# Layer 0 of a four-layer convolution network: an earlier sampling chain, a later copy of the second sum's rows, one more VectorE eviction

## The chip, the cores and the metric

The kernel runs on one core of a Trainium2 chip. The metric is the device time in microseconds (us) of one execution of the whole program, four layers in one launch; the change touches layer 0 alone. Engines are named TensorE (PE, with its weight loads PEld), VectorE (DVE), ScalarE (ACT), GpSimd (POOL) and SyncE (SP, which issues DMAs here).

## The reference

Layer 0 is an attention over sampled keys with a learned position bias, on `x` of shape (2, 512, 32, 32), 8 heads of 64 channels, one group a head:

```python
q = _gconv1x1(xn, qw)
off = tanh(einsum(gelu(depthwise_conv(q) + b), off_pw_w)) * 4.0     # 64 offsets a head
vgrid = grid + off                                                  # where to sample
kv = _grid_sample(xn, vgrid)                                        # bilinear, 64 keys a head
k, v = _gconv1x1(kv, kw), _gconv1x1(kv, vw)
pos = grid_q[:, :, None, :] - grid_kv[:, None, :, :]                # 1024 queries x 64 keys x 2
bias = sign(pos) * log1p(abs(pos))
bias = relu(bias @ cpb_w1 + cpb_b1)                                 # 2 -> 128
bias = relu(bias @ cpb_w2 + cpb_b2)                                 # 128 -> 128
bias = bias @ cpb_w3 + cpb_b3                                       # 128 -> 1
attn = softmax(q^T k * 64**-0.5 + bias)
x = x + out_w @ (attn v);  x = x + mlp(bn2(x))
```

For each of the 16 heads of the two batches, 1024 x 64 positions go through the 128 x 128 layer `cpb_w2`. That is nearly all of layer 0's work. Layers 1 to 3 are other attentions and are the same in both kernels.

## The kernel before

**Units and blocks.** The loop of layer 0 goes over 16 *units* u (a batch and a head), in each over 8 steps o, in each over two halves: 256 *blocks*, written (o,half) below. Two units share one of 8 *pairs* (128 channels); an odd unit is the second of its pair. In a block `first_hidden` (L746) makes four tiles h1 of 128 x 1024 for the **next** block on VectorE (L760), from a buffer that holds two blocks' worth. `second_hidden` (L771) multiplies them by `cpb_w2` on TensorE (L787) into four PSUM tiles of 128 x 1024, called q0 to q3 here. The PSUM pool `ps` has three such tiles, so each one needs the third before it evicted; the transposes of a pair (`tr`, L674) and the attention's output (`o`) take tiles of the same pool.

**Evictions.** ScalarE evicts q0 to q3 with a relu (L801) and scales q0 (L806, with a bias L804). GpSimd then adds the four up: an accumulating DMA y1 += y0 (L811), y3 += y2 (L815), y3 += y1 (L818, one block later, `join`). In some blocks VectorE evicts one tile with the addition in it: q3 in *late* blocks (L796), q2 in *early* ones (L799); in an early block L811 and ScalarE's eviction of q2 fall away, and L806 becomes L804.

**Folds and gathers.** The sum of a step is folded by accumulating DMAs on GpSimd's queue (L821, L843, L846) and *gathered* by two DMAs on SP (`sum<-h`, L853) into `sum0` (even o) or `sum1` (odd o). A unit later these sums are scaled (L222), folded (`keys_rows`, L858 and L861) and copied to the tile `rows` by two DMAs on SP each (`rows<-sum`, L865). `self.refolds` lists all these steps with the block in which each is due, and `refold_more` (L827) takes what is due; its last call in a block (`gather=True`) issues the SP DMAs. The gather of step o is due in block 2o + 5 of the unit, counted from 0, the rows of the first sum in block 6 and those of the second in block 8. In each engine's queue instructions run in the order in which they are issued. On SP the order comes from priorities; a DMA issued inside `self.behind(self.gathered)` stands behind the last gather.

**The attention of the unit before** (`attend`, L905, v = u - 1) starts at block (5,0): VectorE adds `rows` to the scores (L910), transposes, takes maxima, subtracts (L925); ScalarE takes the exponential at the end of block (6,0) (L927); VectorE sums, divides and transposes back (the *division*, L934 and L936) at the end of (7,0); TensorE multiplies by v (L947) at the end of (7,1).

**The next pair's chain** (`offsets`, L401, then `sampled`, L592) makes offsets, reads the sampling spots back from DRAM (`at<-spots`, L495), turns `xT` (L674 and its copy L604), takes distances (L611 on VectorE, L618 and L619 on ScalarE), relus (L623, L624), their product (L626), the sampling matmuls (L633) and keys and values (L647 to L655). It advances by one step, up to its next `yield`, at the end of a block: `self.step(after)` first advances the attention; only where that yields nothing true does `self.step(front)` advance the pair's chain:

```python
                    self.refold_more(i, True)
                    if not self.step(after):
                        self.step(front)
```

So a `yield True` in the attention keeps the pair's chain out of that block. The queues of TensorE, ScalarE, VectorE and GpSimd follow this order exactly.

Of the kernel before, what the change touches and what calls it, by code (L numbers as in the profile page):

```python
# [57 lines left out]
class Net:  # L58
# [40 lines left out]
    def layer0(self):  # L99
# [3 lines left out]
        with ExitStack() as ctx:  # L103
# [45 lines left out]
            with self.tc.manual_schedule(engines=engines):  # L149
# [40 lines left out]
                for i, (u, o, half) in enumerate(quads):  # L190
                    self.half = half
                    if o == 2 and half == 1 and u % 2 == 0 and u // 2 + 1 < BP:
                        nxt = pairs[u // 2 + 1]
                        front += [self.offsets(nxt, u // 2 + 1, ps), self.sampled(nxt, u // 2 + 1, ps)]
                    h1 = ready
                    if i + 1 < len(quads):
                        if quads[i + 1][1:] == (7, 0) and u + 1 < 2 * BP:
                            self.advance(front, lambda: "logs" in pairs[(u + 1) // 2])
                        ready = self.first_hidden(*quads[i + 1], pairs, tables)
                    last_set = u == last and o >= 4  # L200
                    if half == 0:
                        if o == 0:
                            before, sums = sums, []
                        if o % 4 == 0:
                            group = []
                        if i + 2 < len(quads):
                            both = self.two_tiles(f"h2_{u}_{o}3")
                            group.append([both[:, 0, :], both[:, 1, :], both])
                        else:
                            group.append([self.four_rows(f"h2_{u}_{o}{n}3") for n in range(2)])  # L210
                        if o < 2:
                            sums.append(self.four_rows(f"sum{u}_{o}"))
                    self.second_hidden(i, u, o, half, h1, group[-1], i + 1 == len(quads), last_set)
                    if half == 1 and not last_set:
                        end = i + (3 if u == last else 4)
                        self.refolds.append((i + 2, end, end, self.refold(group[-1][2], sums[o % 2], o // 2, u == last)))
                    v = u - 1
                    if half == 0 and o in (1, 2) and 0 <= v < last - 1:
                        z = before[o - 1]
                        if o == 1:  # L220
                            rows = self.soft.tile([P, HF], F32, tag="pt", name=f"rows{v}")
                        nc.scalar.activation(z, z, AF.Copy, scale=self.last_sign)  # L222
                        self.refolds.append((i + 1, i + 4, i + 4, self.keys_rows(z, rows, o - 1)))
                    if half == 1 and o == 2 and v >= 0:
                        sims[v] = ps_s.tile([P, HF], F32, tag="sim", name=f"sim{v}")
                        if v == last - 1:
                            self.sum_product(sims[v], self.thrice, True, before)
                        self.advance(front, lambda: "v" in pairs[v // 2])
                        self.keys_queries(v, pairs[v // 2], sims[v], v < last - 1)
                    if v >= 0 and (o, half) == ((5, 0) if v < last - 1 else (2, 1)):  # L230
                        if v == 8:
                            self.advance(after, lambda: False)
                            att = [apool.tile([P, N], F32, tag=f"att{t}", name=f"att{v}_{t}") for t in range(CT)]
                        after.append(self.attend(v, pairs[v // 2], sims[v], att, ps, rows if v < last - 1 else None))
                        if v % 8 == 7:
                            after.append(self.projection(ps, att, ow, v // 8))
                    elif half == 1 and u == last and o == 5:
                        sims[u] = ps_s.tile([P, HF], F32, tag="sim", name=f"sim{u}")
                        self.sum_product(sims[u], self.twice[:, 16:48], True, sums)
                    elif half == 1 and u == last and o == 7:  # L240
                        self.sum_product(sims[u], self.folded[:, 8:40], False, [one[0] for one in group[:2]])
# [3 lines that stand above are left out]
# [347 lines left out]
    def sampled(self, m, bt, ps):  # L592

        nc = self.nc
        b, t = divmod(bt, CT)
        spots = self.fone.tile([P, 2 * NJ, 2], F32, tag="spots", name=f"at{b}{t}")
        if bt > 0:
            yield  # L600
        self.send(bt == 0, spots, m["spots"].rearrange("k d -> (k d)").partition_broadcast(P))
        if "xT" not in m:
            self.sampling(m, bt)
            nc.scalar.copy(m["xT"], self.turn(m, bt, ps))  # L604
        elif "w" not in m:
            self.sampling(m, bt)
        xnT = m["xT"]
        yield
        wx = self.fone.tile([P, 2 * NJ], F32, tag="wx", name=f"wx{b}{t}")
        w = m["w"]  # L610
        nc.vector.tensor_tensor(  # L611
            w,
            spots[:, :, 1].unsqueeze(1).to_broadcast([P, NB, 2 * NJ]),
            self.ys.unsqueeze(2).to_broadcast([P, NB, 2 * NJ]),
            ALU.subtract,
        )
        yield
        nc.scalar.activation(wx, spots[:, :, 0], AF.Abs, bias=self.grid[:, G_X : G_X + 1])  # L618
        nc.scalar.activation(w, w, AF.Abs)  # L619
        yield  # L620
        yield from self.odd()
        wp = self.bank[:, 384:512]
        nc.scalar.activation(wp, wx, AF.Relu, scale=-1.0, bias=1.0)  # L623
        nc.scalar.activation(w, w, AF.Relu, scale=-1.0, bias=1.0)  # L624
        yield
        nc.vector.tensor_tensor(w, w, wp.unsqueeze(1).to_broadcast([P, NB, 2 * NJ]), ALU.mult)  # L626
        yield
        yield from self.odd()
        kv_ps = self.bank[:, 384:448]
        for n in range(NB):  # L630
            for par in range(2):
                rows = slice(par * DH, (par + 1) * DH)
                nc.tensor.matmul(  # L633
                    kv_ps[rows, :],
                    lhsT=xnT[:, n, rows],
                    rhs=w[:, n, rows],
                    start=(n == 0),
                    stop=(n == NB - 1),
                )
        kv = self.fone.tile([P, NJ], F32, tag="kv", name=f"kv{b}{t}")  # L640
        nc.vector.tensor_copy(kv, kv_ps)
        keys = self.fpool.tile([P, 2, NJ], F32, tag="k", name=f"k{b}{t}")
        nc.gpsimd.memset(keys, 0.0)
        yield
        yield from self.odd()
        k_ps = self.bank[:, 256:320]
        nc.tensor.matmul(k_ps, lhsT=self.l0qkv[:, 1, t, :], rhs=kv, start=True, stop=True)  # L647
        v_ps = self.bank[0:NJ, 384:512]
        nc.tensor.matmul(v_ps, lhsT=kv, rhs=self.l0qkv[:, 2, t, :], start=True, stop=True)
        for par in range(2):  # L650
            rows = slice(par * DH, (par + 1) * DH)
            nc.vector.tensor_scalar(keys[rows, par, :], k_ps[rows, :], DH**-0.5, None, ALU.mult)
        vals = self.fpool.tile([P, P], F32, tag="v", name=f"v{b}{t}")
        nc.vector.tensor_copy(vals[0:NJ, :], v_ps)
        nc.scalar.copy(vals[NJ:P, :], v_ps)  # L655
        m["k"], m["v"] = keys, vals
        yield
# [113 lines left out]
    def second_hidden(self, i, u, o, half, h1, one, final, last_set):  # L771
# [4 lines left out]
        nc = self.nc  # L776
        vec, pool = nc.vector, nc.gpsimd
        late = half == 1 and u > 0 and o in ((1, 2), (1, 2, 3, 4))[u % 2]
        early = half == 1 and 0 < u < 2 * BP - 1 and o in (0, 7)
        ys = []  # L780
        for q in range(4):
            hp = self.ps_h.tile([P, N], F32, tag="ps", name=f"hp_{u}_{o}{half}{q}")
# [43 lines left out]

    def refold_more(self, i, gather=False):  # L827

        going = []
        for at, last, when, fold in self.refolds:  # L830
            if at < last and at <= i and not gather or at == last and when <= i and gather:
                for _ in fold:
                    going.append((at + 1, last, when, fold))
                    break
            else:
                going.append((at, last, when, fold))
        self.refolds = going

    def refold(self, both, to, c, once):

# [14 lines left out]
    def keys_rows(self, z, to, jj):  # L855
# [6 lines left out]
        yield  # L862
        for h in range(2):
            at = h * NJ + jj * 32
            nc.sync.dma_start(to[at : at + 32, :], z[0::4, h * HF : (h + 1) * HF])  # L865

    def sum_product(self, sim, lhsT, start, zs):

# [36 lines left out]
    def attend(self, u, m, sim, att, ps, bias=None):  # L905
# [28 lines left out]
        nc.vector.tensor_tensor(t, t, joint.unsqueeze(2).to_broadcast([P, 2 * NB, W]), ALU.mult)  # L934
        pt = self.soft.tile([P, HF], F32, tag="pt", name=f"pt{u}")
        self.weights_turned = nc.vector.transpose(pt, t.rearrange("p a k -> p (a k)"))  # L936
        yield

        if ps:
            o = ps.tile([P, 2, HF], F32, tag="ps", name=f"o{u}")  # L940
# [1276 lines left out]
```

## Time and profile before

| what | value |
|---|---|
| median of 3 runs | 3203.44 us (3201.72 to 3206.21) |
| the profiled execution | 3206.31 us, its span 3204.6 us |
| loop of layer 0, first to last matmul of L787 | 23.1 to 1883.4 us |
| busy, of the span | PE 99%, DVE 77%, ACT 59%, POOL 74% |
| ScalarE evictions L801 | 950, 1109 ns each |
| VectorE h1 L760 | 1028, 1210 ns each |
| accumulating DMAs L811 | 227, 512 KB each |
| mean granted TensorE clock | 1.000 |

A group's row names line, engine and operation, the tiles out<-in and their shape, the count, then busy time and mean ns, then the idle time of the engine just before and what ended it. A timeline row has start and duration in us, engine, line, operation, tiles and count, and in brackets the idle time before the row and its releaser; `SPq` and `ACTq` are DMAs issued by those engines' queues. TensorE is pipelined: rows give its starts as recorded and its ends as modelled, so a stop is read from the distance of starts.

### The profile page before, as it was taken

How to read it: one execution, taken by the hardware profiler on the slowest of the kernel's cores; microseconds unless marked ns; L12 is line 12 of the kernel's file. 1: busy time of each engine (PE TensorE's matmuls, PEld its weight loads, DVE VectorE, ACT ScalarE, POOL GpSimd, SP SyncE). 2: the span in 40 equal slices, each digit the busy share in tenths (PEclk: the TensorE clock that was granted, in tenths of full speed). 3: DMA queues.
4: the chain of work that ended last, by engine and by line, in shares of the span. 5: the costliest groups of instructions: out<-in, count | busy, mean ns of one | idle time of the engine just before them, and what ended most of it. 6: DMA issues, size and time to landing. Idle time of an engine off the chain costs nothing.

```text
span 3204.6 us, 58752 instructions
## 1 busy us (share of the span) xinstructions
PE 3179.3 (99%) x23956; PEld 1201.3 (37%) x23956; DVE 2471.8 (77%) x2834; ACT 1904.5 (59%) x1985; POOL 2363.7 (74%) x1664
## 2 busy tenths in 40 slices
PE   9999999999999999999999999999999999999999
PEld 4333333233233333233333234444556433455333
DVE  7888988888888688888888766475475689755897
ACT  7887877877787587877777641111221566113662
POOL 7999999999999699999999854342353458534575
PEclk9999999999999999999999999999999999999999
DMA  6797797888878588788878751110000000000001
GB/s 168 162 189 161 156 180 165 162 174 167 164 162 178 101 173 164 162 166 175 165 161 171 163 167 61 40 53 27 1 1 27 14 1 1 15 0 14 1 1 54
DMA packets 96591, 341.92 MB, mean 107 GB/s; under 512 B 19888, under 2 KB 22064, under 8 KB 79216
## 3 DMA queue, kind: packets, MB, share of 16 engines
q0 software_dynamic: 56224, 244.88, 40.1%
q1 hardware_dynamic: 23264, 65.20, 6.1%
q10 hardware_dynamic: 16816, 27.90, 3.2%
q8 instruction: 193, 3.16, 0.4%
q14 instruction: 94, 0.77, 0.1%
HBM read 67.37 MB, written 4.46 MB: 22 GB/s over the span
## 4 chain that ended last, share of the span: by engine, by line
PE 71%; POOL 13%; DVE 9%; DMA 3%; issue 3%; ACT 1%; DVEq 0%; POOLq 0%; ACTq 0%; SPq 0%
PE hp L787 33%; POOL h L818 5%; PE s L1750 5%; PE o L1779 5%; POOL h L815 3%; DVE h L760 3%; DMA h<-h 2%; POOL h L811 2%; PE qk30P L1525 2%; PE qk20P L1525 2%; PE m_0P L1034 1%; PE m_6P L1034 1%; PE m_5P L1034 1%; PE m_3P L1034 1%; PE qk31P L1525 1%
## 5 line engine op out<-in xcount | busy, mean ns | idle before, releaser
L787 PE MATMUL hp<-h,w2s 128*32 128x512 f32 x16384 | 1777.5, 593 | 9.9 <-ACT h L801 5.3
L760 DVE CUSTOM_DVE_ANT_1 h<-tx,bank 128x1024 f32<-128x1024 f32 (+1 forms) x1028 | 1180.6, 1210 | 119.0 <-PE hp L787 80.5
L801 ACT ACTIVATE h<-hp,magb 128x1024 f32<-128x1024 f32 x950 | 1044.9, 1109 | 370.5 <-PE hp L787 314.7
L787 PEld LDWEIGHTS hp<-h,w2s 128*32 128x32 f32 x16384 | 550.2, 110 | 1204.3 <-issue 1100.9
L818 POOL TENSOR_TENSOR h<-h,h 128x1024 f32<-128x1024 f32 x254 | 753.4, 2966 | 35.6 <-DMA h<-h 30.4
L815 POOL TENSOR_TENSOR h<-h,h 128x1024 f32<-128x1024 f32 x209 | 653.7, 3128 | 6.7 <-DVE h L799 5.2
L811 POOL DMA_DIRECT2D h<-h x227 | 316.5, 1394 | 81.4 <-ACT h L801 80.9
L1754 ACT ACTIVATE e<-s 128x1024 f32<-128x1024 f32 x256 | 262.0, 1025 | 181.1 <-PE s L1750 174.2
L1779 PE MATMUL o<-e,v 64*64 64x512 f32 x2048 | 265.2, 589 | 2.2 <-DVE q L1818 2.2
L1750 PE MATMUL s<-q,k 64*64 64x512 f32 x2048 | 265.9, 591 | 0.0
L806 ACT ACTIVATE h<-h,flip 128x1024 f32<-128x1024 f32 x182 | 209.6, 1152 | 6.0
L843 POOL DMA_DIRECT2D h<-h x124 | 182.2, 1469 | 15.6 <-DMA h<-h 11.1
L1761 POOL TENSOR_TENSOR some<-some,e 128x1024 f32<-128x1024 f32 x64 | 167.8, 2621 | 26.6 <-ACT e L1754 24.0
L1759 POOL TENSOR_TENSOR some<-e,e 128x1024 f32<-128x1024 f32 x32 | 76.1, 2379 | 141.3 <-DVE sum L1768 106.2
L821 POOL DMA_DIRECT2D h<-h x127 | 157.4, 1239 | 5.3 <-issue 3.2
L1766 DVE TENSOR_TENSOR sum<-sum,e 128x1024 f32<-128x1024 f32 x64 | 124.0, 1938 | 29.4 <-ACT e L1754 26.7
L846 POOL DMA_DIRECT2D h<-h x120 | 142.9, 1191 | 4.0 <-DMA h<-h 3.3
L1004 POOL TENSOR_TENSOR mlp_w<-mlp_w 128x512 f32<-128x512 f32 x16 | 23.4, 1460 | 159.2 <-DMA mlp_w<-in_mlp_w 132.9
L1779 PEld LDWEIGHTS o<-e,v 64*64 64x64 f32 x2048 | 77.7, 133 | 145.1 <-issue 135.0
L796 DVE SCALAR_TENSOR_TENSOR h<-hp,under,h 128x1024 f32<-128x1024 f32 x46 | 59.1, 1284 | 90.5 <-ACT h L801 75.1
L1750 PEld LDWEIGHTS s<-q,k 64*64 64x64 f32 x2048 | 76.5, 133 | 133.2 <-issue 117.3
L1100 ACT ACTIVATE mh<-mh,cols 128x512 f32<-128x512 f32 x64 | 46.1, 721 | 124.3 <-DVE mh L1118 64.3
(595 smaller groups left out, 3637.6 us busy)
## 6 DMA issues: line engine op xcount, KB each, us to landing
h<-h POOLq DMA_DIRECT2D x354, 512.0 KB, 5.9
h<-h POOLq DMA_DIRECT2D x124, 256.0 KB, 4.7
lb<-logs ACTq DMA_DIRECT2D x47, 512.0 KB, 6.1
mlp_w<-in_mlp_w SPq DMA_DIRECT2D x16, 1024.0 KB, 4.8
h<-h POOLq DMA_DIRECT2D x120, 128.0 KB, 3.8
sum<-h SPq DMA_DIRECT2D x240, 64.0 KB, 3.4
lb<-logs SPq DMA_DIRECT2D x16, 512.0 KB, 7.3
sum<-sum POOLq DMA_DIRECT2D x28, 256.0 KB, 6.2
```

The source lines that it names most:

```text
L760: self.nc.vector._custom_dve(TENSOR_ADD_SAT, out=h1[r][:, k, cut, :], in0=x[:, 4 * half + 2 * r + k, :].unsqueeze(1).to_broadcast([P, H // ...
L787: nc.tensor.matmul(hp[rows, cut], lhsT=self.l0w2[:, 32 * q : 32 * q + 32], rhs=h1[k][:, cut], start=True, stop=True)
L801: nc.scalar.activation(y, hp, AF.Relu, bias=self.magb[:, q, 0:1])
L806: nc.scalar.activation(y, y, AF.Copy, scale=self.flip)
L811: self.added = pool.dma_start(y, ys[0], accum_op=ALU.add)
L815: self.added = (vec if final else pool).tensor_tensor(y, y, ys[2], ALU.add)
L818: (vec if final else pool).tensor_tensor(z, z, other, ALU.add)
L843: nc.gpsimd.dma_start(both[0::4], both[2::4], accum_op=ALU.add)
L1750: nc.tensor.matmul(s[halves[c], par, :], lhsT=ks[p][rows, at : at + DH], rhs=qs[p][rows, cut], start=True, stop=True)
L1754: nc.scalar.activation(e, s, AF.Exp, scale=DH**-0.5)
L1761: nc.gpsimd.tensor_tensor(state["some"], state["some"], e, ALU.add)
L1779: nc.tensor.matmul(o[halves[par], r, :], lhsT=v[n // 2][rows, n % 2, at : at + DH], rhs=e[rows, par, :], start=(n == 0), stop=(n == NB - 1),)
```

## The change

1. In `sampled` the first `yield` of pairs 1 to 7 is gone, so that all its steps come one call earlier. In `attend` the yield after the division is true where the attention's unit is even, that is, in odd units of the loop: there no step of the pair's chain is taken in that block.
2. The copies of the second sum's rows are due half a block later (i + 4.5), which is the next block; what is due in one block is taken in falling order of due time, so that they stand behind the gather of that block, and they are issued inside `behind(self.gathered)`.
3. In the last unit (u = 15) block (0,1) becomes an early block.

```diff
@@ layer0
-                        self.refolds.append((i + 1, i + 4, i + 4, self.keys_rows(z, rows, o - 1)))
+                        self.refolds.append((i + 1, i + 4, i + 4 + (o - 1) / 2, self.keys_rows(z, rows, o - 1)))
@@ sampled
-        if bt > 0:
-            yield
         self.send(bt == 0, spots, m["spots"].rearrange("k d -> (k d)").partition_broadcast(P))
@@ second_hidden
-        early = half == 1 and 0 < u < 2 * BP - 1 and o in (0, 7)
+        early = half == 1 and u > 0 and o in ((0, 7) if u < 2 * BP - 1 else (0,))
@@ refold_more
-        going = []
-        for at, last, when, fold in self.refolds:
-            if at < last and at <= i and not gather or at == last and when <= i and gather:
-                for _ in fold:
-                    going.append((at + 1, last, when, fold))
-                    break
-            else:
-                going.append((at, last, when, fold))
-        self.refolds = going
+        def due(at, last, when, fold):
+            return at == last and when <= i if gather else at < last and at <= i
+
+        now = [e for e in self.refolds if due(*e)]
+        for e in sorted(now, key=lambda e: -e[2]) if gather else now:
+            next(e[3], None)
+        self.refolds = [(e[0] + 1, *e[1:]) if e in now else e for e in self.refolds if not (gather and e in now)]
@@ keys_rows
-            nc.sync.dma_start(to[at : at + 32, :], z[0::4, h * HF : (h + 1) * HF])
+            with self.behind(self.gathered):
+                nc.sync.dma_start(to[at : at + 32, :], z[0::4, h * HF : (h + 1) * HF])
@@ attend
-        yield
+        yield u % 2 == 0
```

## The prediction

> **What bounds the kernel now.** I read the page first, then the engine timelines of single units, then the waits. The words unit, block, pair and q0 to q3 are those of the section on the kernel before.
>
> ```profile
> PE 3179.3 (99%) x23956; PEld 1201.3 (37%) x23956; DVE 2471.8 (77%) x2834; ACT 1904.5 (59%) x1985; POOL 2363.7 (74%) x1664
> L787 PE MATMUL hp<-h,w2s 128*32 128x512 f32 x16384 | 1777.5, 593 | 9.9 <-ACT h L801 5.3
> ```
>
> TensorE runs from end to end, at a granted clock of nine tenths or more in every slice (mean 1.000); layer 0 is the stretch of the 16384 matmuls of L787. So the only thing that this change can win or lose there is time in which TensorE waits, and what counts is how much room the other engines have before TensorE stops for them. Unit 5, on TensorE, ScalarE and VectorE:
>
> ```profile
> 637.17 68.87 PE L787 MATMUL hp<-h,w2s 128*32 128x512 f32 x640
> ...
> 685.51 1.11 ACT L801 ACTIVATE h<-hp,magb 128x1024 f32<-128x1024 f32 x1 [0.56 <-PE hp L787]
> 686.64 1.28 ACT L927 ACT_TABLE_LOAD   x1
> 687.93 0.72 ACT L927 ACTIVATE t<-t,cols 128x512 f32<-128x512 f32 x1
> 688.57 1.10 ACT L801 ACTIVATE h<-hp,magb 128x1024 f32<-128x1024 f32 x1
> ...
> 690.75 3.11 ACT L801 ACTIVATE h<-hp,magb 128x1024 f32<-128x1024 f32 x3
> ...
> 700.25 0.40 ACT L618 ACTIVATE wx<-at,grid 128x128 f32<-128x128 f32 x1
> 700.56 1.05 ACT L619 ACTIVATE sampling<-sampling 128x1024 f32<-128x1024 f32 x1
> 701.51 1.10 ACT L801 ACTIVATE h<-hp,magb 128x1024 f32<-128x1024 f32 x1
> ```
>
> The first row gives TensorE's pace: 640 matmuls are 160 steps of four, the last one 0.59 us long, so (68.87 - 0.59) / 159 = 0.4294 us a step, 1.72 us a PSUM tile and 6.87 us a block. Block (3,0) starts at 637.17; q3 of block (6,1) therefore starts at 637.17 + 7 x 6.87 + 3 x 1.72 = 690.4, and q0 of (7,0) at 692.1. There are three PSUM tiles, so q3 of (6,1) needs q0 evicted: 688.57 + 1.10 = 689.67, room 0.7. And q0 of (7,0) needs q1 evicted: 690.75 + 1.10 = 691.85, room **0.25 us**. After the exponential (with its table load 2.0 us) ScalarE has no gap until q3 of (6,1). This is the tightest place of an odd unit.
>
> **The change part by part.**
>
> *The pair's steps in odd units.* The removed yield brings the steps of `sampled` one call forward; the attention's division then takes the place of one. By the order of the built instructions, in units 3, 5, ..., 13: the read of `at` and the turn of `xT` (L674, L604; pairs 4 to 7) go from block (4,1) to (4,0); L611 on VectorE from behind the h1 of (6,1) to behind that of (5,0); L618 and L619 from the end of (7,0) to the end of (6,0), straight behind the exponential. No instruction is added and TensorE's work stays; even units keep their orders on all four compute engines.
>
> *ScalarE.* L618 and L619 hold ScalarE 701.51 - 700.25 = 1.26 us. At (7,0) the room of q3 of (7,1) covered that. At (6,0) it comes in front of the eviction with 0.25 us of room: TensorE waits 1.26 - 0.25 + 0.05 = 1.06 us (0.05 us is what passes from an eviction's end to the matmul that waits for it: 1802.11 against 1800.94 + 1.11 further down), first 0.6 at q3 of (6,1), the rest at q0 of (7,0). Units 5, 7, 9, 11 and 13 show the same 0.25; unit 3 has 0.12, so 1.19. Sum 5 x 1.06 + 1.19 = **+6.5 us**. Bounds: -1.5 us (the trace has TensorE's weight loads wait 1.5 us in all, five times, behind L619 in its old place, and that goes) to 6 x 1.26 = 7.6. I take 6.5, since both ends of the room are read from rows.
>
> On the table, the Trainium skill says in "ScalarE: Activation LUTs", What ACT_TABLE_LOAD costs, that a switch is 1283 ns of load and some 1380 ns of drain. The rows show the 1.28 and then the exponential 0.01 us behind it, with no drain; the measurement decides. With the page's drain each odd unit would lose 1.38 us more, 6 x 1.38 = 8.3 us, an estimate that I leave out.
>
> *VectorE.* Rows of unit 5:
>
> ```profile
> 664.94 1.28 DVE L796 SCALAR_TENSOR_TENSOR h<-hp,under,h 128x1024 f32<-128x1024 f32 x1 [2.34 <-ACT h L801]
> 666.14 4.61 DVE L760 CUSTOM_DVE_ANT_1 h<-tx,bank 128x1024 f32<-128x1024 f32 x4
> ...
> 673.38 4.62 DVE L760 CUSTOM_DVE_ANT_1 h<-tx,bank 128x1024 f32<-128x1024 f32 x4 [0.16 <-DVE bank L743]
> ...
> 684.48 1.22 DVE L611 TENSOR_TENSOR sampling<-at,bank 128x1024 f32<-128x1024 f32 x1
> ```
>
> L611 (1.2 us) now runs at 666.2, between the first two of these rows (the h1 of (5,1) is the second, that of (6,0) the third); the idle 2.34 us lies before L796 and cannot take it, and from there to its old place VectorE is dense. The h1 of (6,0) ended at 678.00; TensorE needs the fourth tile one step after the block's start, 678.39 + 0.43 = 678.8. Room 0.8, so 1.2 - 0.8 + 0.06 = +0.46 us. In unit 3 the same group ends at 446.09 + 4.61 = 450.70 for a need at 451.0: room 0.3, +0.96. Units 7 to 13 have 1.47 or more, nothing. Sum **+1.4 us**, bounds 0 and 6 x 1.2 = 7.2. The read of `at` lands 2.9 to 6.0 us after its issue; issued behind q3 of (4,0), about 657.5, it is there by 663.5, in time for 666.2.
>
> *The turn.* In unit 11 ScalarE's q3 of (4,0) waits for a gather's landing, and TensorE for that tile:
>
> ```profile
> 1376.93 3.64 PE L787 MATMUL hp<-h,w2s 128*32 128x512 f32 x32 [0.36 <-ACT h L801]
> 1380.50 1.09 PE L674 MATMUL tr<-ident,xn 128*128 128x128 f32 x8
> 1381.52 7.07 PE L787 MATMUL hp<-h,w2s 128*32 128x512 f32 x63
> ```
>
> The turn (1.16 us of TensorE) takes a PSUM tile. Done in (4,0) it runs before the wait, but TensorE then meets the late tile after q0 of (4,1) instead of after q1: 1.16 - 1.72 = 0.55 us sooner, so the wait of 0.5 grows to 1.06. Units 7 and 11 show that wait, 9 and 13 have the room: **+1.1 us**, bounds 0 and 4 x 0.55 = 2.2. The gather itself is issued by rows that do not move, so I expect it late as before.
>
> *Pair 1 (units 1, 2).* The 16 matmuls of L633 go from unit 2 to (4,1) of unit 1, L626 with them. TensorE's sum is the same 1.2 us; unit 1 already shows about 0.75 us of waits at (6,1) and (7,1), which that pause moves rather than removes, and L618 and L619 at (3,0) have 0.7 us of room. Zero, bounds -0.7 and +0.6.
>
> *The second sum's rows.* SP issues them behind the gather of o = 2 instead of ahead of it.
>
> ```profile
> 1000.70 1.13 SPq L865 DMA_DIRECT2D rows<-sum  x2
> 1010.12 1.15 SPq L853 DMA_DIRECT2D sum<-h  x2
> ...
> 1015.64 0.71 DVE L910 TENSOR_TENSOR sim<-sim,rows 128x512 f32<-128x512 f32 x1
> ```
>
> The gather gains nothing: it is issued 8.3 us after the rows here and 3.4 us or more in every unit, held by its own fold (the queue's waits: 1334.2 us for `h<-h`). The rows' cover shrinks: issued at 1011.4 and landing as before 4.0 us later, they are there at 1015.4, 0.2 us ahead of L910, and behind L910 lies another 0.9 us of room of the h1. In unit 11 they come 0.3 us ahead of a VectorE that L611 has delayed. Zero; with the slowest landing of the rows, 6.3 us, about +1.7 in such a unit, so up to +5 for three units.
>
> *The last unit.* Of block (0,1) L811's DMA (1.67 us of POOL, 0.85 of it not under the add in progress) and one ScalarE eviction (1.1) go; L799 on VectorE (1.28) comes, where VectorE idles over 2 us per block.
>
> ```profile
> 1785.14 1.67 POOL L811 DMA_DIRECT2D h<-h  x1
> ...
> 1800.94 1.11 ACT L801 ACTIVATE h<-hp,magb 128x1024 f32<-128x1024 f32 x1 [6.12 <-DMA h<-h]
> ...
> 1802.11 1.92 PE L787 MATMUL hp<-h,w2s 128*32 128x512 f32 x16 [2.89 <-ACT h L801]
> ```
>
> TensorE loses 3.1 us at this row and 0.5 and 0.7 at its next two stops, 4.3 in all (each start against the steps before it), behind a POOL that has had nearly no gap for 30 us and DMAs that take up to 9.8 us. POOL 0.85 us earlier is the least; all 4.3 the most, since 512 KB leave the DMA engines just before. I take **-2.0**, nearer the least, because the DMA that ends the wait is the next one, still to be made.
>
> **Sum**: 6.5 + 1.4 + 1.1 + 0 + 0 - 2.0 = +7.0 us. The profiled execution took 3206.31 us (span 3204.6 and 1.7 around it) and would take 3213.3; it stands 2.9 us above the median of the runs, so against the median 3203.44 + 7.0 = 3210.4, and I say 3210.5, 0.2% slower. About 0.2% (6.4 us) is what a measurement of this kernel can tell from no change.
>
> **Rivals.** (a) *ScalarE's pair of steps is covered*: TensorE does not stop at (7,0). For it: TensorE's starts are recorded, its ends are modelled. Against it: in unit 1 ScalarE is 0.75 us further behind at that very place, and block (6,1) takes 0.5 us longer. Then 7.0 - 6.5 = +0.5, 3204 us, not slower; it decides once the room at q0 of (7,0) is 1.2 us instead of 0.25. (b) *The last unit clears entirely*: -4.3 instead of -2.0 gives +4.7, 3208 us; for it the 9.8 us of one DMA, against it the POOL order that stays. (c) *The rows come too late for L910*: +3 to +5 more, 3214 to 3216 us; for it the 0.2 us of cover in unit 8, against it a median landing of 3.9 us. (d) *The change does more than its rows show*, for instance the gather of o = 1 lands earlier and the waits at (4,1) of units 3, 7 and 11 (2 us) go, with (a) and (b) true: 3204 - 2.3 - 2 - 1.1, some 3198 us.
>
> **How the numbers follow.** Forecast or worse (3209.8 and up, (c) in it) 0.60; (a) 0.18 and (b) 0.15, within 0.2%, together 0.33; (d) 0.07, at or beyond the edge on the fast side. The range goes from 3201.5, where (a) meets part of (b), to 3218, the forecast with the VectorE term at its upper bound or (c).
>
> **What the profile after would show.** Right: in units 3 to 13 L618 directly behind the exponential, and TensorE waiting some 1.1 us for evictions between q3 of (6,1) and q0 of (7,0); in units 3 and 5 a wait for h1 at (6,0); in unit 15 the wait at (2,0) some 2 us shorter. Wrong: blocks (6,1) of odd units still 6.87 us long, or VectorE idle before L910. The sum would be wrong above all if those stops fall where TensorE would have waited anyway, for instance before the attention's product at the end of the unit.

## The result, and the profile after

The changed kernel takes 3215.69 us (median of 7 runs, 3212.94 to 3218.68) against 3205.64 us (7 runs, 3201.72 to 3207.97) for the kernel before: a ratio of 1.0033, 95% interval 1.0022 to 1.0045. It is slower by 10 us (7 to 14); 7 were forecast. The time stated, 3210.5 us, is 5.2 below the measured one, and 2.2 of that come from the starting point: the working started from a median of 3203.44 over three runs, which over seven is 3205.64. The line numbers of the changed kernel are two to four lower: L787 is now L785, L801 L799, L611 L609, L618 and L619 L616 and L617, L674 L672, L796 L794, L853 L849, L865 L862, L910 L907, L927 L924.

The page of the kernel after, busy times and the row of the large matmuls:

```profile
PE 3186.7 (99%) x23956; PEld 1201.3 (37%) x23956; DVE 2477.7 (77%) x2835; ACT 1903.8 (59%) x1984; POOL 2361.2 (74%) x1663
L785 PE MATMUL hp<-h,w2s 128*32 128x512 f32 x16384 | 1784.7, 593 | 10.4 <-DVE h L797 4.7
```

The counts are those of the change: one VectorE instruction more, one fewer on ScalarE and on GpSimd. The span grows from 3204.6 to 3212.4 us, and nothing of that is in layers 1 to 3: from the last matmul of layer 0 on, both profiled executions take 1321.1 us. So the table below lists how long each of some units lasts, from the start of its first matmul to the start of the next unit's; for unit 15 to the start of its last. The last two columns are the stops of block (6,1), its length less the 6.87 us of 16 steps.

| unit | before | after | (6,1) before | (6,1) after |
|---|---|---|---|---|
| 1 | 112.72 | 113.93 | 0.5 | 0 |
| 2 | 115.14 | 114.89 | 0 | 0 |
| 5 | 112.05 | 115.79 | 0 | 1.84 |
| 7 | 113.73 | 115.06 | 0 | 1.8 |
| 9 | 141.67 | 143.67 | 0 | 1.82 |
| 11 | 113.79 | 116.12 | 0 | 1.8 |
| 13 | 113.22 | 115.43 | 0 | 1.8 |
| 15 | 117.58 | 112.79 | 0 | 0 |

Every odd unit from 3 to 13 stops 1.8 us in block (6,1). Unit 9 shows it with no wait for a DMA beside it. First ScalarE's timeline of the kernel after (start, duration, then engine, line and tiles):

```profile
1180.19 1.12 ACT L799 ACTIVATE h<-hp,magb 128x1024 f32<-128x1024 f32 x1 [0.54 <-PE hp L785]
1181.32 1.28 ACT L924 ACT_TABLE_LOAD   x1
1182.62 0.72 ACT L924 ACTIVATE t<-t,cols 128x512 f32<-128x512 f32 x1
1183.24 0.41 ACT L616 ACTIVATE wx<-at,grid 128x128 f32<-128x128 f32 x1
1183.55 1.04 ACT L617 ACTIVATE sampling<-sampling 128x1024 f32<-128x1024 f32 x1
1184.50 1.10 ACT L799 ACTIVATE h<-hp,magb 128x1024 f32<-128x1024 f32 x1
```

and TensorE's of the same unit:

```profile
1164.41 20.89 PE L785 MATMUL hp<-h,w2s 128*32 128x512 f32 x181
1185.65 1.92 PE L785 MATMUL hp<-h,w2s 128*32 128x512 f32 x16 [0.35 <-ACT h L799]
1187.83 7.50 PE L785 MATMUL hp<-h,w2s 128*32 128x512 f32 x68 [0.26 <-ACT h L799]
```

L616 and L617 stand straight behind the exponential, as forecast, and the eviction behind them ends at 1184.50 + 1.10 = 1185.60; 0.05 us later TensorE starts q3 of (6,1). The starts of its steps put 1.36 us of stop there and 0.44 at q0 of (7,0) (1187.83 - 1185.65 = 2.18 for four steps of 0.43). Forecast was 1.06 for both. The other 0.75 us is VectorE's, which its rows of unit 9 show, after:

```profile
1158.69 1.28 DVE L794 SCALAR_TENSOR_TENSOR h<-hp,under,h 128x1024 f32<-128x1024 f32 x1 [3.53 <-ACT h L799]
1159.89 1.21 DVE L609 TENSOR_TENSOR sampling<-at,bank 128x1024 f32<-128x1024 f32 x1
1161.02 4.61 DVE L758 CUSTOM_DVE_ANT_1 h<-tx,bank 128x1024 f32<-128x1024 f32 x4
...
1168.43 4.62 DVE L758 CUSTOM_DVE_ANT_1 h<-tx,bank 128x1024 f32<-128x1024 f32 x4 [0.16 <-DVE bank L741]
```

and before:

```profile
1151.34 1.28 DVE L796 SCALAR_TENSOR_TENSOR h<-hp,under,h 128x1024 f32<-128x1024 f32 x1 [2.34 <-ACT h L801]
1152.54 4.61 DVE L760 CUSTOM_DVE_ANT_1 h<-tx,bank 128x1024 f32<-128x1024 f32 x4
```

In this unit the turn pauses TensorE for 1.17 us. Before, the pause came behind q3 of (4,1), the tile that L796 evicts: VectorE had its eviction done and won 1.17 us for the h1 that follow. Now it comes ahead of that tile; L794 waits 3.53 us instead of 2.34, and the pause is lost to VectorE. At the same place L609 moves the h1 back by another 1.13 us (1161.02 - 1159.89). Read as in the prediction, from the end of the fourth tile to the recorded start of the second step of its block, the h1 of (6,0) had 2.0 us of room before; after, the tile ends 0.5 us later than that start (1168.43 + 4.62 = 1173.05 against 1172.55).

TensorE's recorded starts do not yet show that loss in (6,0) (0.15 us there). It is seen in ScalarE's rows, the one above and these from before:

```profile
1173.10 1.11 ACT L801 ACTIVATE h<-hp,magb 128x1024 f32<-128x1024 f32 x1 [0.57 <-PE hp L787]
1174.23 1.28 ACT L927 ACT_TABLE_LOAD   x1
```

The exponential's table load starts 1181.32 - 1179.14 = 2.18 us after the recorded start of (6,1), against 1174.23 - 1172.82 = 1.41 before. The eviction ahead of it waits for TensorE in both, so its matmuls end 0.77 us later than their recorded starts let one expect. The 1.36 us at q3 is this 0.77 and the 0.59 of ScalarE.

The turn's other side, unit 11 on TensorE after:

```profile
1381.28 1.09 PE L672 MATMUL tr<-ident,xn 128*128 128x128 f32 x8
1382.30 1.92 PE L785 MATMUL hp<-h,w2s 128*32 128x512 f32 x16
1385.08 25.51 PE L785 MATMUL hp<-h,w2s 128*32 128x512 f32 x233 [0.85 <-ACT h L799]
```

The stop is now one PSUM tile behind the turn and has grown as forecast: 1385.08 - 1382.30 - 1.72 = 1.06 us, after 0.5.

The second sum's rows in unit 5, SP's queue after:

```profile
654.82 15.75 SPq L849 DMA_DIRECT2D sum<-h  x4
670.68 1.24 SPq L862 DMA_DIRECT2D rows<-sum  x2
```

and VectorE behind it:

```profile
675.85 0.70 DVE L907 TENSOR_TENSOR sim<-sim,rows 128x512 f32<-128x512 f32 x1 [1.61 <-DMA rows<-sum]
```

The rows stand behind both gathers and go out at 670.68. With edit 1 alone, where the first five units take as long (573.6 us in both), they go out 7.7 us earlier:

```profile
663.00 1.12 SPq L863 DMA_DIRECT2D rows<-sum  x2
```

VectorE is idle for them, and the unit takes 1.9 us more than with edit 1 alone (115.79 against 113.86).

The last unit, TensorE after:

```profile
1778.48 41.41 PE L785 MATMUL hp<-h,w2s 128*32 128x512 f32 x384
1819.70 1.04 PE L870 MATMUL sim<-sum,signed 128*32 128x512 f32 x8
```

Six blocks without a stop: the 4.75 us that unit 15 had lost there in the profile of before are gone. By the profiles alone that would be the change's largest effect. The experiments show that most of it is not.

### The profile page after: what moved, and what is told of

Its sections match the earlier page's. It is cut to its first block, busy times and chain, and to the rows that moved or that the text cites. A ratio compares the mean times of both kernels' runs of the same rounds, so it can differ in the third digit from the quotient of the medians.

```text
span 3212.4 us, 58705 instructions
## 1 busy us (share of the span) xinstructions
PE 3186.7 (99%) x23956; PEld 1201.3 (37%) x23956; DVE 2477.7 (77%) x2835; ACT 1903.8 (59%) x1984; POOL 2361.2 (74%) x1663
## 4 chain that ended last, share of the span: by engine, by line
PE 74%; DVE 14%; POOL 6%; ACT 2%; issue 2%; DMA 1%; SPq 0%; DVEq 0%; ACTq 0%; POOLq 0%
PE hp L785 36%; DVE h L758 6%; PE s L1747 5%; PE o L1776 5%; POOL h L816 2%; POOL h L813 2%; PE qk20P L1522 2%; PE qk30P L1522 2%; PE qk21P L1522 1%; PE m_7P L1031 1%; PE m_4P L1031 1%; PE m_3P L1031 1%; PE m_2P L1031 1%; PE m_0P L1031 1%; PE qk31P L1522 1%
## 5 line engine op out<-in xcount | busy, mean ns | idle before, releaser
L785 PE MATMUL hp<-h,w2s 128*32 128x512 f32 x16384 | 1784.7, 593 | 10.4 <-DVE h L797 4.7
L799 ACT ACTIVATE h<-hp,magb 128x1024 f32<-128x1024 f32 x949 | 1044.6, 1108 | 383.5 <-PE hp L785 350.2
L785 PEld LDWEIGHTS hp<-h,w2s 128*32 128x32 f32 x16384 | 549.5, 110 | 1212.7 <-issue 1115.5
L809 POOL DMA_DIRECT2D h<-h x226 | 296.8, 1313 | 98.9 <-ACT h L799 96.6
L839 POOL DMA_DIRECT2D h<-h x124 | 183.4, 1479 | 7.6 <-DMA h<-h 4.4
L819 POOL DMA_DIRECT2D h<-h x127 | 156.7, 1234 | 5.2 <-issue 3.1
L842 POOL DMA_DIRECT2D h<-h x120 | 140.4, 1170 | 3.2 <-DMA h<-h 2.0
L794 DVE SCALAR_TENSOR_TENSOR h<-hp,under,h 128x1024 f32<-128x1024 f32 x46 | 59.1, 1284 | 89.5 <-ACT h L799 74.3
```

The costliest lines, as they stand in the source:

```text
L785: nc.tensor.matmul(hp[rows, cut], lhsT=self.l0w2[:, 32 * q : 32 * q + 32], rhs=h1[k][:, cut], start=True, stop=True)
L799: nc.scalar.activation(y, hp, AF.Relu, bias=self.magb[:, q, 0:1])
L809: self.added = pool.dma_start(y, ys[0], accum_op=ALU.add)
L839: nc.gpsimd.dma_start(both[0::4], both[2::4], accum_op=ALU.add)
```

## The experiments

Two theories were to be told apart. A: the stops of the odd units come from edit 1 itself, from ScalarE's two steps and from h1 tiles that have become just in time. B: the late rows of edit 2 make VectorE late, and the stops follow from that. Ratios are to the kernel before on the same chip. Line numbers shift by one or two from run to run as well; the row's operation and tiles tell which line of before it is.

### Edit 1 alone

```diff
-        if bt > 0:
-            yield
         self.send(bt == 0, spots, m["spots"].rearrange("k d -> (k d)").partition_broadcast(P))
...
         self.weights_turned = nc.vector.transpose(pt, t.rearrange("p a k -> p (a k)"))
-        yield
+        yield u % 2 == 0
```

> Edit 1 alone (first yield of sampled gone, the division's yield true in odd units). Theory A, the odd units pay for L618 and L619 beside the exponential and for the h1 that L611 delays: blocks (6,1) of units 3 to 13 take 1.8 us more as in the profile after, some 10.9 us in all, the waits of unit 15 stay (4.7 us), so +9 to +12 us against before. Theory B, the late rows of the second sum start the chain in odd units: with the rows in their old place (6,1) takes 1.1 us more at most, and the sum is +4 to +7 us.

Measured: 3216.82 us, ratio 1.0032 (1.0020 to 1.0043). Block (6,1) of all six odd units is 1.80 to 1.83 us too long, and VectorE never waits for the rows. So a loss as large as the whole change's is there without edit 2: theory A holds, and B falls as the cause of the stops at (6,1).

### Edit 2 alone

With the new `refold_more`, whose rewriting is not repeated here:

```diff
-  self.refolds.append((i + 1, i + 4, i + 4, self.keys_rows(z, rows, o - 1)))
+  self.refolds.append((i + 1, i + 4, i + 4 + (o - 1) / 2, self.keys_rows(z, rows, o - 1)))
...
-            nc.sync.dma_start(to[at : at + 32, :], z[0::4, h * HF : (h + 1) * HF])
+            with self.behind(self.gathered):
+                nc.sync.dma_start(to[at : at + 32, :], z[0::4, h * HF : (h + 1) * HF])
```

> Edit 2 alone (second sum's rows behind the next gather). Theory A: VectorE waits for the rows at L910 in a few units, 0.3 to 1.6 us each, of which the room of 0.3 to 0.9 us behind it covers part: +1 to +3 us, in units 2, 3 and 5 above all. Theory B: +4 to +7 us, spread over the odd units.

Measured: 3212.33 us, ratio 1.0018 (1.0009 to 1.0026), some 6 us. That is not nothing, and theory A's figure was too small. The view of the tile `rows` in this kernel lists what VectorE was idle for ahead of L909, its line of L910 (us, times):

```profile
its engine sat idle before it (us, times) until:
  DMA rows<-sum: 9.8, 7
  issue: 2.4, 3
```

In the three that the view calls "issue" the rows also landed 0.08 us before L909's start, so ten of the fourteen attentions wait for their rows, 12.2 us in all. The kernel before has no such wait. TensorE passes a part on, for instance in unit 5 0.91 us at (6,0) and 0.57 at (6,1), after 1.96 us of VectorE's waiting. Where all of the 6 us go is not shown: the profiled execution is the fastest of its twelve (3207.05 us), and up to the last matmul of layer 0 it is only 1.1 us longer than the profile of before, and 2.8 longer than that of the kernel before once more (below). In the changed kernel the same view has less:

```profile
  DMA rows<-sum: 2.7, 2
  issue: 2.3, 3
```

Five waits, 5.0 us in all, in units 1, 2, 3, 5 and 14. In the odd units edit 1 has put L609 ahead of L907, so that VectorE comes later itself; units 7 to 13, of which five waited with edit 2 alone, wait no longer than 0.07 us.

### Edit 3 alone

```diff
-  early = half == 1 and 0 < u < 2 * BP - 1 and o in (0, 7)
+  early = half == 1 and u > 0 and o in ((0, 7) if u < 2 * BP - 1 else (0,))
```

> Edit 3 alone (block (0,1) of unit 15 evicts q2 on VectorE). If the gain in the last unit is its own, TensorE's 4.7 us of waits in blocks (1,0) to (2,1) of unit 15 go and the time falls by 4 to 5 us, faster than before by 0.15%. If it comes from the pauses of the earlier units, which give GpSimd time to catch up, -2 us at most.

Measured: 3205.70 us, ratio 0.9998 (0.9989 to 1.0007). There is no gain that the runs can show, though the profiled execution was 3.4 us shorter in its span. Unit 15 took 114.63 us; TensorE still stops in block (2,1):

```profile
1765.23 38.30 PE L787 MATMUL hp<-h,w2s 128*32 128x512 f32 x352
1804.82 3.64 PE L787 MATMUL hp<-h,w2s 128*32 128x512 f32 x32 [1.29 <-ACT h L801]
```

### The kernel before once more

To see which stops belong to the kernel and which to one execution, the kernel before was run again, unchanged.

> The kernel before with nothing changed but a comment, to see which of its stops are the kernel's and which the execution's. Theory A: the 4.75 us of stops at (1,0), (2,0) and (2,1) of unit 15 are one execution's; here unit 15 takes 113.5 to 116.5 us, and the stop of 1.1 us in unit 6 and those at (4,1) differ too. Rival: unit 15 takes 117 us or more again; then the stops belong to the kernel, and edit 3 alone has removed 3 us that the medians do not show. Ratio 1.000 either way.

Measured: ratio 0.9999 (0.9989 to 1.0008). Unit 15 took 114.46 us, not 117.58:

```profile
1767.45 37.97 PE L787 MATMUL hp<-h,w2s 128*32 128x512 f32 x352
1806.90 3.64 PE L787 MATMUL hp<-h,w2s 128*32 128x512 f32 x32 [1.47 <-ACT h L801]
```

Theory A held. Over the eight profiles without edit 3 unit 15 takes 114.63 us in the mean (seven of them 113.96 to 114.74, the eighth is the 117.58 on which the prediction was made); over the three with it 113.63 (112.79, 113.46 and 114.63). So three of the 4.75 us were that execution's. What edit 3 is worth is at most about 1 us and not shown: by itself it gave the 114.63, no less than without it, and the two shorter ones have edit 1 as well.

### Edit 1 with ScalarE kept free

Against edit 1 alone, the exponential's yield is here the true one in odd units instead of the division's, so that L618 and L619 stay at (7,0); the turn and L611 come early as in edit 1.

```diff
         nc.scalar.activation(t, t, AF.Exp, bias=self.col("cpb_b3"))
-        yield
+        yield u % 2 == 0
...
         self.weights_turned = nc.vector.transpose(pt, t.rearrange("p a k -> p (a k)"))
-        yield u % 2 == 0
+        yield
```

> Edit 1 with another block left out: the attention keeps the pair's chain from the exponential's block (6,0) in odd units, not from the division's (7,0). L611 and the turn stand as after, L618 and L619 as before, no other edit. Theory A (ScalarE): with nothing beside the exponential the stop of 1.06 us at (7,0) goes; VectorE's part of some 0.75 us a unit stays, so +1 to +5 us against before. Rival (VectorE alone, by L611 and the turn): (6,1) keeps its 1.8 us in each odd unit, +9 us or more.

Measured: 3210.09 us, ratio 1.0009 (1.0000 to 1.0018), against 1.0032 with all of edit 1. On ScalarE the eviction again follows the exponential (unit 9):

```profile
1179.44 0.73 ACT L925 ACTIVATE t<-t,cols 128x512 f32<-128x512 f32 x1
1180.08 1.09 ACT L799 ACTIVATE h<-hp,magb 128x1024 f32<-128x1024 f32 x1
...
1191.77 0.41 ACT L616 ACTIVATE wx<-at,grid 128x128 f32<-128x128 f32 x1
1192.08 1.04 ACT L617 ACTIVATE sampling<-sampling 128x1024 f32<-128x1024 f32 x1
```

Block (6,1) is 0.55 us too long, and (7,1), which was 0.71 us too long before (the attention's product stands there), is 0.94 too long: 0.55 + 0.23 = 0.78 us are left of 1.81. ScalarE's two steps therefore cost 1.03 us a unit, and the rival that VectorE alone is the cause falls.

### Edit 1 with the turn kept late

Against edit 1 alone, the turn goes back to (4,1); the read of the spots stays at (4,0) and L611 at (5,0).

```diff
         self.send(bt == 0, spots, m["spots"].rearrange("k d -> (k d)").partition_broadcast(P))
+        if bt > 0:
+            yield
         if "xT" not in m:
             self.sampling(m, bt)
             nc.scalar.copy(m["xT"], self.turn(m, bt, ps))
...
         xnT = m["xT"]
-        yield
+        if bt == 0:
+            yield
```

> Edit 1, but with the turn of xT (and its copy by ScalarE) in its old place, block (4,1); only the read of the sampling spots, the distances on VectorE and the two steps on ScalarE come early. Theory A: the move of the turn takes from VectorE the 1.17 us of TensorE's pause in which it gains room for the h1 of (5,1) and (6,0). With the turn back, units 7, 9, 11 and 13 have that room again (0.7 + 1.2 and 0.3 + 1.2, less the 1.2 of the distances step), and their block (6,1) is 1.1 us too long (ScalarE's share alone) instead of 1.82, while units 3 and 5, which turn nothing, keep 1.8. The stop at (4,1) of unit 11 is 0.5 again instead of 1.09. In all 4 x 0.75 + 0.6 = 3.6 us less than edit 1: some 3213, ratio 1.0020 to 1.0024. Rival: the 0.76 us comes from the early distances step alone, whatever the turn does; then (6,1) stays at 1.8 in all six odd units and the time at 3216 to 3217, ratio 1.0032.

Measured: 3212.92 us, ratio 1.0019 (1.0010 to 1.0028). Block (6,1) is 1.05 us too long in units 9 and 13, 1.17 in unit 11 and 1.45 in unit 7; units 3 and 5, which turn nothing, keep 1.82 and 1.80. TensorE in unit 9:

```profile
1156.87 25.96 PE L788 MATMUL hp<-h,w2s 128*32 128x512 f32 x240
1183.23 1.93 PE L788 MATMUL hp<-h,w2s 128*32 128x512 f32 x16 [0.40 <-ACT h L802]
1185.42 10.08 PE L788 MATMUL hp<-h,w2s 128*32 128x512 f32 x92 [0.26 <-ACT h L802]
```

By the steps' starts the stops are 0.59 us at q3 of (6,1) and 0.46 from there to q0 of (7,0), the forecast's 0.6 and "the rest" of 1.06. With the turn in its old place the room of the h1 is 1.25 and 0.87 us in unit 9, and nothing of VectorE's step reaches TensorE. Theory A held. Units 7 and 11 keep 0.40 and 0.12 us more; the room of their h1 of (6,0) is only 0.05 and 0.31 us, less than the 0.43 of one step. What that step has to do with it is said below; why unit 7 has so little room is open.

### The turn alone

Against the kernel before, only the read of the spots and the turn come one call earlier.

```diff
-        if bt > 0:
-            yield
         self.send(bt == 0, spots, m["spots"].rearrange("k d -> (k d)").partition_broadcast(P))
...
         xnT = m["xT"]
         yield
+        if bt > 0:
+            yield
```

> The kernel before with only the read of the spots and the turn of xT one call earlier; the distances and the two steps on ScalarE keep their old places. Theory A: the room of the h1 of (5,1) and (6,0) in units 7 to 13 falls from 1.85 to 2.4 and 1.47 to 2.0 us to the 0.7 and 0.3 of unit 3, with no stop there, since nothing is put in front of them; the stops at (4,1) of units 7 and 11 grow by up to 0.55 each. 0 to +1.5 us, 3206 to 3207.5, ratio 1.0000 to 1.0005. Rival: the room stays above 1.4, then the turn is not what took it.

Measured: 3205.92 us, ratio 0.9999 (0.9989 to 1.0008). The room of the h1 of (5,1) and (6,0) in units 7, 9, 11 and 13 falls from 1.85 to 2.4 and 1.47 to 2.0 us to 1.20 and 0.81 in all four, the figures of unit 5, which turns nothing (1.20 and 0.81 before); the 0.7 and 0.3 expected were unit 3's. In units 9 and 13 that is the 1.2 us of the pause. Alone it costs nothing that the runs show, though unit 11 stops 1.6 us at (4,1) in the profile (unit 7 does not).

### Edit 1 with neither cost

The exponential's yield true in odd units instead of the division's, and the turn late; of the edit only L611's early place (and the read ahead of it) is left. Against the kernel before:

```diff
         nc.scalar.activation(t, t, AF.Exp, bias=self.col("cpb_b3"))
-        yield
+        yield u % 2 == 0
...
-        if bt > 0:
-            yield
         self.send(bt == 0, spots, m["spots"].rearrange("k d -> (k d)").partition_broadcast(P))
+        if bt > 0:
+            yield
         if "xT" not in m:
...
         xnT = m["xT"]
-        yield
+        if bt == 0:
+            yield
```

> Edit 1 with both of its costs taken away as far as the runs so far name them: the exponential's yield is the true one in odd units (so the two steps on ScalarE stay at (7,0)), and the turn stays in (4,1); what is left of the edit is the distances step on VectorE at (5,0). Theory A (the costs are ScalarE's 1.05 us per odd unit and the room that the turn's move takes, and they add up): block (6,1) of units 9, 11 and 13 is 6.87 us long again, with at most 0.3 us too much in unit 7; units 3 and 5 keep 0.5 to 0.6 there. In all +1 to +2 us, 3206 to 3208, ratio 1.0002 to 1.0007. Rival: the early distances step costs by itself; then (6,1) is 0.5 us too long and (7,1) 0.2 in all six units, and the time is that of edit 1 with the exponential's yield, 3209 to 3211, ratio 1.0009.

Measured: 3207.09 us, ratio 1.0002 (0.9993 to 1.0011). Unit 9 is back at 141.66 us and unit 13 at 113.22, the lengths of before. In unit 9 there is no stop in six blocks:

```profile
1153.25 41.41 PE L788 MATMUL hp<-h,w2s 128*32 128x512 f32 x384
```

Units 3 and 5 keep 0.57 and 0.55 us at (6,1). The rival (the early step costs by itself, in all six units) falls: it does so only in units 3 and 5, where nothing is turned. With both costs taken away 0.6 us (-2 to 4) are left of edit 1's 10.

### The changed kernel without edit 2

Against the changed kernel (with the old `refold_more`):

```diff
-  self.refolds.append((i + 1, i + 4, i + 4 + (o - 1) / 2, self.keys_rows(z, rows, o - 1)))
+  self.refolds.append((i + 1, i + 4, i + 4, self.keys_rows(z, rows, o - 1)))
...
-            with self.behind(self.gathered):
-                nc.sync.dma_start(to[at : at + 32, :], z[0::4, h * HF : (h + 1) * HF])
+            nc.sync.dma_start(to[at : at + 32, :], z[0::4, h * HF : (h + 1) * HF])
```

> The changed kernel with the copies of the second sum's rows in their old place (edits 1 and 3). Theory A: within the changed kernel the late rows cost little beside edit 1, because where VectorE waits for them in odd units the stop at (6,1) is mostly the same stop: 3215 to 3217, ratio 1.0028 to 1.0034. Rival: the costs add up, then it is faster than the changed kernel by what edit 2 alone costs, 5 to 6 us: 3210 to 3211, ratio 1.0015.

Measured: 3214.81 us, ratio 1.0027 (1.0018 to 1.0036). The changed kernel's 1.0033 lies inside that interval, so the runs do not tell how much of edit 2's 0.18% is left beside edit 1. In the profiles the units with the long waits, 1, 2 and 5, take 341.7 us together here and 344.6 in the changed kernel, 2.9 more. But unit 3 takes 1.6 less there (114.07 against 115.63): a stop of 1.5 us in (4,1), which stands here, is missing in the changed kernel:

```profile
433.93 30.71 PE L785 MATMUL hp<-h,w2s 128*32 128x512 f32 x272 [1.25 <-ACT h L799]
```

Up to the last matmul of layer 0 the changed kernel's profile is 1.0 us longer than this one's; whether edit 2 costs more than that beside edit 1 stays open.

No kernel of these beat the one before.

## Why the prediction was right or wrong

Direction and main cause were right, and the sum was 3 us short: terms of 7.0 us against 10.0 measured. The prediction named two signs of being wrong; one of them, VectorE idle before L910, is there in five attentions. Point by point:

**The pair's steps, ScalarE: +6.5 was right.** Where nothing of VectorE's is mixed in, the stop is at the forecast place, in the forecast parts (0.59 and 0.46 us in unit 9 with the turn late), 1.05 us a unit where VectorE is out of the way; taken away, it brings 1.03 back. Six units give 6.3 us. Rival (a), that the step is covered, fell. The Trainium skill ("ScalarE: Activation LUTs", What ACT_TABLE_LOAD costs) adds a drain of some 1380 ns to the load of a table. It is not in the trace after either: in unit 9 the eviction ahead ends at 1180.19 + 1.12 = 1181.31, the load takes 1181.32 to 1182.60, and the exponential starts at 1182.62; the measurement decides. The prediction's estimate of 8.3 us for it would not have been a cost of this change anyway, since the load stands at the same place in both kernels.

**VectorE: +1.4 was mis-sized, and this is the step that failed.** It said that units 7 to 13 "have 1.47 or more, nothing". That room was read from the trace of before, where the turn stands behind (4,1); the next term of the same sum moved the turn. With the turn in (4,0) the room in all four is 0.81 us, as in unit 5, and the 1.2 us of L611 do not fit. So units 5 to 13 lose 0.76 to 0.78 us each and unit 3 1.1: 5.0 us in all. The term for these four is 4 x 0.78 = 3.1 of the 3.6 us that were missing. The other 0.5 is size: in unit 5 0.46 was forecast and 0.76 measured, in unit 3 0.96 and 1.1. The term's upper bound, 7.2, had held it.

A second misreading explains these sizes: the room was read to one step after the block's start. The loop around L787 goes over the four h1 tiles innermost, and four matmuls start together in each step; if each of the four reads another tile, the fourth tile is wanted with the first step, 0.43 us sooner. Then a room r as read above costs 0.43 - r where that is positive. In unit 5 the early L611 leaves r = 0.81 - 1.13 = -0.32, so 0.75 (0.76 measured); with the turn late unit 7 has r = 0.05, so 0.38 (0.40), unit 11 0.31, so 0.12 (0.12), units 9 and 13 0.87, so nothing (nothing). Unit 3 had less than 0.43 to begin with and pays nearly all of the 1.13 (1.1). No run was made to test this; it is read from the loop, and it fits the runs that there are.

**The turn: +1.1, not settled.** The mechanism was right in unit 11 (0.5 to 1.06 us, as worked out). In unit 7 there was no stop after, and 0.38 in unit 13, so the profiled sum is nearly unchanged; these stops depend on when a gather lands, and the kernel before alone moves them by 0.2 to 0.3 us between two executions (unit 7 0.51 and 0.29, unit 11 0.56 and 0.90). Over the five profiles with the turn early units 7, 11 and 13 stop there 1.7 us together in the mean, over the six with it late 1.0. That difference is of the forecast's sign, but single units differ by more than it from profile to profile.

**Pair 1: 0 was right.** In edit 1 alone units 1 and 2 together take 227.90 us, before 227.86.

**The rows: 0 was wrong.** Alone, edit 2 costs 6 us (3 to 8). The working took the cover from unit 8, 0.2 us, with the median landing, and went from there to nothing. The median itself leaves half of the landings later, and unit 8 is not the tightest: in the trace of before L910 starts 5.5 us after the gather's issue there, but 5.1 in unit 5, 5.0 in unit 14 and 4.6 in unit 3, where the same working (1.3 to the rows' issue, 4.0 to their landing) leaves no cover at all. Rival (c) is thus partly true: rows that come late cost edit 2 alone more than its +3, but beside edit 1 the cost is not settled, 2.9 us in units 1, 2 and 5 and 1.0 over layer 0.

**The last unit: -2.0 was too much.** The stops on which it was sized were for the most part one execution's: by the profiles edit 3 is worth 1 us at most, and its runs alone allow -3.5 to +2.2. Rival (b) looked true in the profile of after, where no stop is left, but does not hold: with edit 3 alone the stop at (2,1) stays, and without it unit 15 takes only 1.2 to 2.0 us more than the 112.79 in seven profiles of eight.

The measured terms of edit 1 are 6.3 + 5.0 = 11.3 us, and its own runs say 10 (6 to 14). The whole change has 10 (7 to 14) too, so what edits 2 and 3 add to it nearly cancels or is too small for these runs. The two profiled executions differ by 7.8 us only, because the one of before has the 3 us of stops in unit 15 that do not come again. The direction did not come by luck: the ScalarE term alone gives it, and that is the term which the runs bear out.

## What to carry to other kernels

When two edits of one change touch the same unit, read the room for the one from a trace in which the other is already made, or subtract it: a pause of the busiest engine gives the others room only if it falls behind the instruction that they were waiting for. Look up in the source which matmul reads the last tile before a room is read to a recorded start. A stop that ends with a DMA should not be sized from a single execution; profile the unchanged kernel twice, and what does not repeat is not the kernel's. A copy that is moved behind another DMA of its queue must be costed in every unit and by its latest landing, not in one unit by the median.

## What the runs showed of the hardware

Where only engines decide, a unit repeats to a hundredth: unit 5 of the kernel before took 112.05 and 112.06 us, unit 9 141.67 and 141.66, unit 13 113.22 both times. Where a DMA's landing decides, the same program differs by microseconds: unit 12 115.51 and 117.04, unit 15 117.58 and 114.46. In the longer unit 12 ScalarE's queue stood still for a gather:

```profile
1462.42 1.11 ACT L801 ACTIVATE h<-hp,magb 128x1024 f32<-128x1024 f32 x1 [3.55 <-DMA sum<-h]
```

TensorE's mean clock was 1.000 in all of these profiles.

TensorE's recorded starts can hide a lag: when the last h1 tile came late, block (6,0) of unit 9 looked 0.15 us late by its starts, and the eviction that waited for its matmuls was 0.77 us late.
